# Attention: four of ten chunks of probabilities turned in 32x32 squares by VectorE and put in place by transfers on chip

## The chip, the cores and the metric

The kernel runs on one core of a Trainium2 chip, in fp32 throughout. The metric is the device time of one execution in microseconds (us). The time before is 2645.14 us, the median of three runs (2643.16 to 2648.54). Five engines work side by side, each with a queue of its own: TensorE (PE, with its weight loads as PEld), VectorE (DVE), ScalarE (ACT), GpSimd (POOL) and SyncE (SP), which here only issues transfers (DMAs). They meet in semaphores.

## The reference

A layer norm, then attention and a feed-forward layer with low-rank additions, summed onto the input:

```python
B, S, H = 4, 512, 1024;  NH, NKV, D = 32, 8, 128;  G = NH // NKV        # G = 4
xn = layernorm(x)
q, k, v = split(xn @ w_qkv)                    # 32 query heads, 8 key/value heads
scores = einsum('bqhgd,bkhd->bhgqk', q, k) * D ** -0.5
bias = where(rel >= 0, -slopes * sqrt(rel), -inf)     # causal, by the root of the distance
attn = softmax(scores + bias)
out = einsum('bhgqk,bkhd->bqhgd', attn, v)
x = x + out @ w_o + (xn @ W.T + b + routed_low_rank(xn))
```

What matters here is that `attn` is computed with the queries on the partitions (the softmax sums over keys, along the free dimension), while the product with `v` sums over keys and so wants the keys on the partitions. The probabilities have to be turned.

## The kernel before

There are three stages. `project` makes q, k and v (its two outer levels of products use fewer multiplications by sums of blocks) and leaves them in HBM. `attend` does the attention. `finish` multiplies by `w_o` and `W`, takes the low-rank part and the input in, and writes out. This change is in `attend`, which runs from about 1115 to 1842 us of the profiled span.

**Units.** `attend` goes through 32 units `u = (p, h, bi)`: a pair of batch entries, a key/value head, one of the two entries. In a unit four query heads (`G`) are handled together. The 512 queries are four tiles of 128 (`i` = 0 to 3), and because of the causal mask tile `i` needs only the keys of tiles `j` = 0 to `i`. So there are 4 + 3 + 2 + 1 = 10 chunks `(i, j)` in a unit; each is 128 queries by 128 keys for four heads, 128 x 512 numbers.

**Steps.** `scores(u, i)` multiplies q and k on TensorE into a bank of PSUM (L1014). VectorE adds the bias and finds the extreme (L1019), ScalarE takes the exponential with its sum (L1023), VectorE inverts the sum (L1026) and GpSimd scales the probabilities in place (L1028). They lie in `p0` to `p3`, two buffers each. `transpose_probs(u, i)` turns every chunk of tile i: four turns on TensorE (L1039), 128 x 128 each, into one PSUM bank, and one copy to a `pt` buffer, by VectorE for even j (L1042) and by ScalarE for odd j (L1044). `weigh(u, i)` multiplies the turned chunks with v (L1052), and ScalarE copies the result to `o` (L1053).

**Order.** The loop over units runs one unit ahead with the scores. In the loop of unit u, TensorE does, for i = 3, 2, 1, 0, the scores of tile i of the *next* unit, then (for i = 1 and 0) the weighing of tile i + 2 of u, then the turns of tile i of u. At i = 2 it also turns the next unit's v (`values`, L1003). At the end come the weighings of tiles 1 and 0. TensorE's order is the order of the program (`manual_schedule(engines={PE})`). On the other engines, SP's queue included, a scheduler orders the instructions by its own estimate of when each can run; only instructions in `pin` keep their order among themselves.

**Transfers.** SP's queue issues for each unit the loads of k, q and v two units ahead (L973 to L975) and, spread over two units, the stores of `o`, of sums of `o` and of `ot` for the last stage (`middle_sums`, L1105 to L1119). The sums `os` and `ot` are made by VectorE and GpSimd (L130, L133).

**Buffers.** SBUF is laid out by hand: `counts` and `sizes` name how many buffers of which size a tag has, one if nothing is said. `homes[0]` is the first home of the next stage's operands; it is open already while the attention runs, and its tile `s1` (5 x 256 numbers on each partition) is not in use by then.

Of the kernel before, what the change touches and what calls it, by code (L numbers as in the profile page):

```python
# [12 lines left out]
F32 = mybir.dt.float32  # L13
# [8 lines left out]
P = 128  # L22
NH, NKV, D = 32, 8, 128
G = NH // NKV
# [41 lines left out]
def kernel(  # L66
# [13 lines left out]
    nc = tc.nc  # L80
    B, S, H = x.shape
# [5 lines left out]
    HS = S // 2  # L87
    SCALE = D ** -0.5
    KB = 5
# [850 lines left out]
            assert not (soon or later or weights or quiet or any(apart))  # L940


    def attend(front, begin):


        early = pool("bq", side="right")
        with ExitStack() as stack:
            sb, sq = None, early.__enter__()
            units = [(p, h, bi) for p in range(NP) for h in range(NKV) for bi in range(2)]
            sizes = {"dist": (S,), "q": (G, S), "k": (S,), "vT": (S,), "bias": (G, S)}  # L950
            counts = {"q": 2, "k": 2, "vT": 2, "v": 2, "pt": 10, "o": 4, "ot": 2}
            for i in (3, 2, 1, 0):
                sizes[f"p{i}"] = (G, (i + 1) * P)
                counts[f"p{i}"] = 2
            sizes.update(v=(NT, D), pt=(S,), os=(3, 2, S), o=(G, S), ot=(9, HS))
            queries = ("dist", "q", "k", "vT", "bias")

            def buf(tag, name):
                where = sq if tag in queries else sb
                return where.tile([P, *sizes[tag]], F32, tag=tag, name=name, bufs=counts.get(tag, 1))  # L960

            Q, K, VT, V, PR, O, bias = {}, {}, {}, {}, {}, {}, {}

            def label(u):
                return "_".join(str(k) for k in u)

            def load(u, queue=nc.sync):
                p, h, bi = u
                n = label(u)
                K[u] = buf("k", f"k_{n}")  # L970
                Q[u] = buf("q", f"q_{n}")
                VT[u] = buf("vT", f"vT_{n}")
                queue.dma_start(out=K[u], in_=k_d[2 * p + bi, h - h % 2][:, h % 2])  # L973
                queue.dma_start(out=Q[u], in_=q_d[2 * p + bi, h])
                queue.dma_start(out=VT[u], in_=v_d[2 * p + bi, h - h % 2][:, h % 2])  # L975
# [11 lines left out]
                out=dist, in_=dist, compare_op=ALU.is_ge, fill=FAR,  # L987
# [10 lines left out]
            def values(u):  # L998
                n = label(u)
                V[u] = buf("v", f"v_{n}")  # L1000
                tr = bank("tr", f"v_{n}")
                for t in range(NT):
                    nc.tensor.transpose(tr[:, ts(t, P)], VT[u][:, ts(t, P)], ident)  # L1003
                nc.scalar.copy(V[u], tr.rearrange("p (t d) -> p t d", d=D))

            def scores(u, i):
                p, h, bi = u
                n = (i + 1) * P
                m = f"{label(u)}_{i}"
                tot = sb.tile([P, G], F32, tag=f"tot{i}", name=f"tot_{m}", bufs=2)  # L1010
                pr = PR[u, i] = buf(f"p{i}", f"p_{m}")
                for g in range(G):
                    sc = bank("sc", f"{m}_{g}")
                    nc.tensor.matmul(  # L1014
                        sc[:, :n], Q[u][:, g, ts(i, P)], K[u][:, :n], start=True, stop=True
                    )

                    low = sb.tile([P, 1], F32, tag=f"low{g}", name=f"low_{m}_{g}", bufs=2)
                    nc.vector.tensor_tensor_reduce(  # L1019
                        pr[:, g], sc[:, :n], bias[p, h][:, g, S - n :], -SCALE, BIG,  # L1020
                        ALU.add, ALU.min, low,
                    )
                    nc.scalar.activation(  # L1023
                        pr[:, g], pr[:, g], AF.Exp, bias=low, scale=-1.0, accum_out=tot[:, g : g + 1]
                    )
                nc.vector.reciprocal(tot, tot)  # L1026
                for g in range(G):
                    nc.gpsimd.tensor_scalar(  # L1028
                        pr[:, g], pr[:, g], tot[:, g : g + 1], 1.0, ALU.mult, ALU.mult
                    )  # L1030

            PT, OS = {}, {}

            def transpose_probs(u, i):
                for j in range(i + 1):
                    m = f"{label(u)}_{i}_{j}"
                    tr = bank("tr", m)
                    for g in range(G):
                        nc.tensor.transpose(tr[:, ts(g, P)], PR[u, i][:, g, ts(j, P)], ident)  # L1039
                    pt = buf("pt", f"pt_{m}")  # L1040
                    if j % 2 == 0:
                        nc.vector.tensor_copy(pt, tr)  # L1042
                    else:
                        nc.scalar.copy(pt, tr)  # L1044
                    PT[i, j] = pt
# [95 lines left out]

            for tag in "ot os o p3 p2 p1 p0 v pt".split():
                buf(tag, f"lay_{tag}")
            for i in (3, 2, 1, 0):
                scores(units[0], i)
                if i == 3:
                    values(units[0])
            for n, u in enumerate(units):
                p, h, bi = u
                nxt = units[n + 1] if n + 1 < len(units) else None  # L1150
                after = units[n + 2] if n + 2 < len(units) else None
                if after:
                    load(after)
                if n == len(units) - 6:
                    front[0]()
                if not nxt:
                    early.__exit__(None, None, None)
                    front[1](O[p, h, 0])
                    fill = begin()
                if bi == 1:  # L1160
                    beside.append(middle_sums(p, h, (1, 2), "o", O[p, h, 0], True))
                for i in (3, 2, 1, 0):
                    if nxt:
                        scores(nxt, i)
                    if i > 1:
                        aside(outer, 1)
                    aside(below, 2)
                    if i < 2 or not nxt and i < 3 or n == close - 2 and i == 2:
                        aside(beside, 2)
                    if i < 2:  # L1170
                        weigh(u, i + 2)
                        if i == 0 and not nxt:
                            outer_sums(p, h, slice(HS, S))
                        next(fill, None)
                    transpose_probs(u, i)
                    next(fill, None)
                    if i == 2 and nxt:
                        values(nxt)
                    if i == 3:
                        aside(outer, 1)  # L1180
                    if not nxt:
                        if i == 3:
                            aside(beside, 2)
                        if i == 2:
                            while beside:
                                aside(beside, 1)
                        if i < 2:
                            front[3 - i]()
                if after and after[2] == 0:
                    distances(after)  # L1190
                aside(beside, 2)
                weigh(u, 1)
                next(fill, None)
                weigh(u, 0)
                if n == close:

                    while beside:
                        aside(beside, 1)
                for _ in fill:
                    pass  # L1200
                if bi == 1:
                    if n + 1 == close:
                        o = O[p, h, 1]
                        outer.append(outer_steps(p, h))
                        aside(outer, 1)
                        t = OS[p, h]
                    else:
                        o, t = outer_sums(p, h, slice(0, HS if (p, h) == last else S))
                        beside.append(pause(3))
                        for k in range(2):  # L1210
                            O.pop((p, h, k))
                        OS.pop((p, h))
                    below.append(middle_sums(p, h, (7, 4), "o", o, False))
                    beside.append(middle_sums(p, h, (5, 6, 3), "os", t, False))
# [427 lines left out]
    homes, begun = [], {}  # L1642
# [36 lines left out]
    with tc.manual_schedule(engines={PE, SP}):  # L1679
        attention = attend(  # L1680
            (
                lambda: bring(0, "w", *QUARTERS[:3]), second_home,
                lambda: (ops[1].weights(1), ops[1].weights(2)), lambda: ops[1].tokens(1),
            ),
            begin,
        )
        project(lambda: next(attention))
    with tc.manual_schedule(engines={PE}):
# [42 lines left out]
```

## Time and profile before

| what | value |
| --- | --- |
| median of three runs | 2645.14 us (2643.16 to 2648.54) |
| profiled execution, its own device time | 2642.97 us |
| its span, from the first to the last instruction | 2641.2 us |
| granted TensorE clock, mean | 0.999 |
| TensorE turns of probabilities (L1039) | 1280, 167.6 us busy |
| VectorE copies of turned chunks (L1042) | 192, 683 ns each |
| data moved by transfers | 656.19 MB, 248 GB/s over the span |

How to read such lines: in the list of busy time each engine has its busy microseconds, its share of the span and its number of instructions. In the table of stretches come the stretch, its length, the busy time and instructions (x) of PE, PEld, DVE, ACT and POOL, the granted clock, the share of the transfer engines in use and GB/s. A line of groups is: source line, engine, operation, what is written <- what is read, shape, count, then busy us and mean ns of one, then the idle time of the engine just before them and who ended it. A line of waits reads "who waited <- for whom: us in total, times, longest". A line of a timeline is: start, length, engine, source line, operation; "SPq" is SP's queue, and its length is the time that the issue held SP, not the time of the transfer. A matmul in fp32 shows as two instructions, a turn as one. The busy time of TensorE's groups is modelled at the ends, so neighbouring groups overlap by some tenths of a microsecond.

### The profile page before, as it was taken

To read this page: it belongs to the slowest core of one execution; us is meant where nothing else is said; L and a number is where in the kernel's file an instruction comes from. 1 tells how busy PE (TensorE), PEld (TensorE's weight loads), DVE (VectorE), ACT (ScalarE), POOL (GpSimd) and SP (SyncE) were. 2 spreads that over 40 slices of the span, in tenths; PEclk is the share of its full clock that TensorE was granted. 3 is DMA by queue.
4 is the path that set the end of the run, shared out by engine and by line. 5 is a ranking of instruction groups with operands and counts; after the bars stand their busy time and mean duration, and the time that the engine had idled before them with its cause. 6 is when DMAs were issued, how large, how long until landed. Compare 5 with 4: busy or idle time off the path is not lost.

```text
span 2641.2 us, 35979 instructions
## 1 busy us (share of the span) xinstructions
PE 2592.3 (98%) x11872; PEld 2069.8 (78%) x11872; DVE 1799.8 (68%) x3654; ACT 651.7 (25%) x1730; POOL 1924.0 (73%) x1976
## 2 busy tenths in 40 slices
PE   7999999999999999999999999999999999999999
PEld 6888888888888888856666665656788888888887
DVE  7776867867676677656666666676766666656574
ACT  3111111100000000366766766665000000000000
POOL 3687888877898988666877777684765566755593
PEclk9999999999999999999999999999999999999999
DMA  4479897869876776436566666757987878878884
GB/s 148 135 268 309 305 316 258 275 200 330 275 261 216 240 255 207 144 105 223 189 222 215 209 223 195 233 208 240 369 276 285 310 294 318 296 275 310 308 329 164
DMA packets 386570, 656.19 MB, mean 248 GB/s; under 512 B 22441, under 2 KB 291113, under 8 KB 376274
## 3 DMA queue, kind: packets, MB, share of 16 engines
q1 hardware_dynamic: 314322, 566.47, 61.8%
q10 hardware_dynamic: 70752, 82.85, 9.7%
q0 software_dynamic: 1312, 4.59, 0.5%
q8 instruction: 95, 1.56, 0.2%
q14 instruction: 89, 0.73, 0.1%
HBM read 392.72 MB, written 261.10 MB: 248 GB/s over the span
## 4 chain that ended last, share of the span: by engine, by line
PE 67%; POOL 3%; DVE 3%; DMA 2%; issue 1%; SPq 0%; ACT 0%; POOLq 0%; DVEq 0%; ACTq 0%
PE pc L1310 16%; PE psc L1014 9%; PE po L1052 9%; PE pd L1310 8%; PE pc_q L553 6%; PE pa L1310 4%; PE pc_kv L553 3%; PE ptr L1039 3%; PE pd_q L553 3%; PE pd_kv L553 2%; PE pa_q L553 1%; DVE p L1019 1%; DVE pt L1042 1%; PE pa_kv L553 1%; DMA s<-os 1%
## 5 line engine op out<-in xcount | busy, mean ns | idle before, releaser
L1028 POOL TENSOR_SCALAR p<-p,tot 128x256 f32<-128x256 f32 (+3 forms) x512 | 320.5, 648 | 136.8 <-DVE tot L1026 87.3
L1014 PE MATMUL psc<-k,q 128*128 128x512 f32 (+3 forms) x1024 | 306.2, 437 | 3.4 <-DVE low L1019 2.1
L1019 DVE CUSTOM_DVE_ANT_0 p<-psc,bias 128x256 f32<-128x256 f32 (+3 forms) x512 | 244.6, 490 | 93.6 <-PE psc L1014 71.2
L1023 ACT ACTIVATE p<-p,low 128x256 f32<-128x256 f32 (+3 forms) x512 | 283.8, 555 | 74.6 <-DVE low L1019 61.3
L1052 PE MATMUL po<-pt,v 128*128 128x512 f32 x640 | 290.9, 593 | 0.5 <-DVE pt L1042 0.5
L133 POOL TENSOR_TENSOR t<-w 128x640 f32<-128x640 f32 x95 | 186.3, 1961 | 135.6 <-DMA w<-m 58.9
L1014 PEld LDWEIGHTS psc<-k,q 128*128 128x128 f32 x1024 | 172.6, 190 | 102.7 <-issue 54.3
L133 POOL TENSOR_TENSOR t<-w,t 128x640 f32<-128x640 f32 x95 | 197.3, 2077 | 34.2 <-PE pc L1310 30.5
L1039 PEld LDWEIGHTS ptr<-ident,p 128*128 128x128 f32 x1280 | 147.3, 141 | 71.4 <-issue 40.1
L1052 PEld LDWEIGHTS po<-pt,v 128*128 128x128 f32 x640 | 116.6, 190 | 109.6 <-issue 99.6
L133 POOL TENSOR_TENSOR wr<-wr 128x256 f32<-128x256 f32 x220 | 173.1, 789 | 33.2 <-DMA wr<-in_w_o_dram 10.3
L1042 DVE COPY pt<-ptr 128x512 f32<-128x512 f32 x192 | 130.0, 683 | 75.8 <-PE ptr L1039 73.8
L1039 PE MATMUL ptr<-ident,p 128*128 128x128 f32 x1280 | 167.6, 274 | 4.3 <-DVE pt L1042 2.9
L553 PE MATMUL pc_q<-xi,ti_q 128*128 128x256 f32 x640 | 165.7, 381 | 2.9 <-DVE q L130 1.8
L168 ACT COPY m<-pc 128x256 f32<-128x256 f32 x30 | 11.2, 373 | 562.7 <-PE pc L1310 488.7
L133 DVE TENSOR_TENSOR wr<-wr 128x256 f32<-128x256 f32 x220 | 141.8, 645 | 7.6 <-DMA wr<-in_w_o_dram 4.0
L133 POOL TENSOR_TENSOR ti_q<-w_q 128x256 f32<-128x256 f32 x128 | 106.1, 829 | 56.0 <-PE pc_kv L553 32.9
L553 PEld LDWEIGHTS pc_q<-xi,ti_q 128*128 128x128 f32 x640 | 119.6, 190 | 24.5 <-issue 7.8
L553 PE MATMUL pd_q<-xi,ti_q 128*128 128x256 f32 x448 | 116.0, 381 | 5.6 <-POOL ti_q L133 5.6
L1310 PE MATMUL pc<-sa,w 128*128 128x256 f32 x480 | 113.8, 385 | 4.5 <-DMA sa<-s 4.5
L168 ACT COPY q<-pc_q 128x256 f32<-128x256 f32 x64 | 23.8, 372 | 357.1 <-PE pc_q L553 309.1
L1310 PE MATMUL pd<-s,w 128*128 128x256 f32 x480 | 111.5, 379 | 0.4 <-DVE s L133 0.4
(343 smaller groups left out, 6003.5 us busy)
## 6 DMA issues: line engine op xcount, KB each, us to landing
sa<-s SPq DMA_DIRECT2D x98, 640.0 KB, 8.1
s<-ot SPq DMA_DIRECT2D x107, 384.0 KB, 4.8
m<-wr SPq DMA_DIRECT2D x70, 512.0 KB, 4.7
w<-m SPq DMA_DIRECT2D x28, 1280.0 KB, 7.2
w_q<-in_w_qkv_dram SPq DMA_DIRECT2D x16, 2048.0 KB, 12.2
q<-q SPq DMA_DIRECT2D x32, 1024.0 KB, 7.2
s<-os SPq DMA_DIRECT2D x45, 512.0 KB, 4.8
t<-wr SPq DMA_DIRECT2D x40, 512.0 KB, 4.2
```

The lines of the kernel that those rows point to most:

```text
L133: return eng.tensor_tensor(dst, u, v, ALU.subtract)
L168: nc.scalar.copy(dst, src)
L553: nc.tensor.matmul(dst, ops_w[m][:, c, :], XI[i][m][:, c, :], start=start and c == 0, stop=c == 1, skip_group_check=True,)
L1014: nc.tensor.matmul(sc[:, :n], Q[u][:, g, ts(i, P)], K[u][:, :n], start=True, stop=True)
L1019: nc.vector.tensor_tensor_reduce(pr[:, g], sc[:, :n], bias[p, h][:, g, S - n :], -SCALE, BIG, ALU.add, ALU.min, low,)
L1023: nc.scalar.activation(pr[:, g], pr[:, g], AF.Exp, bias=low, scale=-1.0, accum_out=tot[:, g : g + 1])
L1028: nc.gpsimd.tensor_scalar(pr[:, g], pr[:, g], tot[:, g : g + 1], 1.0, ALU.mult, ALU.mult)
L1039: nc.tensor.transpose(tr[:, ts(g, P)], PR[u, i][:, g, ts(j, P)], ident)
L1042: nc.vector.tensor_copy(pt, tr)
L1052: nc.tensor.matmul(po, V[u][:, j, :], PT[i, j], start=(j == 0), stop=(j == i))
L1310: nc.tensor.matmul(bk, w[:, k], x[:, k], start=start and k == 0, stop=stop and k == KB - 1, skip_group_check=True,)
```

## The change

Four of the ten chunks of a unit no longer go through TensorE: `(3, 0)`, `(3, 2)`, `(2, 0)` and `(2, 2)`. All four were copied out of PSUM by VectorE. Instead `turn_apart` has VectorE turn each 32 x 32 square of the chunk where it stands, from `p` into a tile `px` (borrowed from `s1` in `homes[0]`; one buffer, shared by tiles 3 and 2). That leaves every square turned inside, but the squares of a 128 x 128 block still stand in the old places. `place_apart` moves the squares: for each pair (a, b) of four groups of 32 partitions, one transfer on SP's queue, from the partitions of a in `px` to those of b in `pd3` or `pd2`: 16 transfers of 32 partitions x 1 KB, each with both chunks and all heads. `weigh` then reads the chunk in `pd` in runs of 32 numbers; v and the sums are as before. The buffers `pt` fall from ten to six, and `pd3` and `pd2` (4 KB a partition each, one buffer each) take their room.

For tile 2 of unit u, both steps come after TensorE's turns at i = 3 of the same loop; it is weighed at i = 0. For tile 3 of the next unit, the turn comes at i = 1 and the placing at i = 0 of the loop before; it is weighed at i = 1 of its own loop. The first unit's tile 3 is done ahead of the loop.

```diff
-    def attend(front, begin):
+    def attend(front, begin, homes):
...
-            counts = {"q": 2, "k": 2, "vT": 2, "v": 2, "pt": 10, "o": 4, "ot": 2}
+            counts = {"q": 2, "k": 2, "vT": 2, "v": 2, "pt": 6, "o": 4, "ot": 2}
...
+            apart = {3: (0, 2), 2: (0, 2)}
+            SQ = 32
+            for i, js in apart.items():
+                sizes[f"pd{i}"] = (P // SQ, len(js), G, SQ)
...
-            PT, OS = {}, {}
+            PT, OS, ahead = {}, {}, {}
+
+            def turn_apart(u, i):
+
+                js = apart[i]
+                px = homes[0].tile([P, KB, HS], F32, tag="s1", name=f"px_{label(u)}_{i}")
+                px = px.rearrange("p k c -> p (k c)")[:, : len(js) * S].rearrange(
+                    "p (b n g i) -> p b n g i", n=len(js), g=G, i=SQ
+                )
+                for n, j in enumerate(js):
+                    nc.vector.transpose(
+                        out=px[:, :, n],
+                        in_=PR[u, i][:, :, ts(j, P)].rearrange("p g (b c) -> p b g c", c=SQ),
+                    )
+                ahead[u, i] = px
+
+            def place_apart(u, i):
+                px = ahead.pop((u, i))
+                pd = buf(f"pd{i}", f"pd{i}_{label(u)}")
+                for a in range(P // SQ):
+                    for b in range(P // SQ):
+                        nc.sync.dma_start(
+                            out=pd[ds(b * SQ, SQ), a], in_=px[ds(a * SQ, SQ), b]
+                        )
+                for n, j in enumerate(apart[i]):
+                    ahead[u, i, j] = pd[:, :, n].rearrange("p a g i -> p g a i")
 
             def transpose_probs(u, i):
                 for j in range(i + 1):
+                    if (u, i, j) in ahead:
+                        PT[i, j] = ahead.pop((u, i, j))
+                        continue
...
                 scores(units[0], i)
                 if i == 3:
                     values(units[0])
+                if i == 2:
+                    turn_apart(units[0], 3)
+                    place_apart(units[0], 3)
...
                     transpose_probs(u, i)
+                    if i == 3:
+                        turn_apart(u, 2)
+                        place_apart(u, 2)
+                    if nxt and i == 1:
+                        turn_apart(nxt, 3)
+                    if nxt and i == 0:
+                        place_apart(nxt, 3)
```

More of the change, by code (lines that the diff above doesn't have):

```diff
@@ L1143, in attend @@
                 buf(tag, f"lay_{tag}")
+            for i in apart:
+                buf(f"pd{i}", f"lay_pd{i}")
             for i in (3, 2, 1, 0):
@@ L1684 @@
             ),
-            begin,
+            begin, homes,
         )
```

## The prediction

> **What bounds the kernel now.** I read the page's busy shares first, then busy time by stretch for the attention stage (1120 to 1840 us) and two of its loops, then who waited for whom on TensorE there, then the groups of the turned lines, then the timelines of TensorE and of SP's queue.
>
> ```profile
> PE 2592.3 (98%) x11872; PEld 2069.8 (78%) x11872; DVE 1799.8 (68%) x3654; ACT 651.7 (25%) x1730; POOL 1924.0 (73%) x1976
> ...
> 1120.00:1840.00 720.00, 712.81 (x3029) 436.35 (x3028) 485.99 (x1431) 483.43 (x1337) 521.35 (x616) 1.00 0.63 205
> 1413.63:1436.46 22.83, 22.64 (x98) 13.90 (x97) 17.11 (x49) 14.59 (x41) 13.86 (x21) 1.00 0.84 265
> 1436.46:1459.31 22.85, 22.71 (x97) 13.84 (x96) 13.84 (x44) 16.60 (x45) 21.11 (x19) 1.00 0.46 151
> ...
> PE ptr L1039 <- DVE pt L1042: 2.9, 15, 0.2
> PE psc L1014 <- DVE low L1019: 2.1, 4, 0.9
> ```
>
> TensorE is busy 99% of the attention stage and waits 5.0 us in 720. A loop over one unit takes 22.84 us and is TensorE's own work end to end; there are 32. So time taken off TensorE is gained, as long as nothing else needs more than the shortened loop.
>
> ```profile
> L1039 PE MATMUL ptr<-ident,p 128*128 128x128 f32 x1280 | 167.6, 274 | 4.3 <-DVE pt L1042 2.9
> L1042 DVE COPY pt<-ptr 128x512 f32<-128x512 f32 x192 | 130.0, 683 | 75.8 <-PE ptr L1039 73.8
> ...
> 1439.89 2.22 PE L1039 MATMUL ptr<-ident,p 128*128 128x128 f32 x16
> 1441.94 2.75 PE L1014 MATMUL psc<-k,q 128*128 128x384 f32 x8
> 1444.53 1.47 PE L1039 MATMUL ptr<-ident,p 128*128 128x128 f32 x12
> 1445.95 0.66 PE L1003 MATMUL ptr_v<-ident,vT 128*128 128x128 f32 x4
> ```
>
> Sixteen turns (i = 3) take 1439.89 to 1441.94, 2.05 us; twelve (i = 2) take 1.42 us. SP's queue in a loop of the same kind:
>
> ```profile
> 1428.91 0.36 SPq L1118 DMA_DIRECT2D s<-os  x1
> 1429.32 0.51 SPq L1119 DMA_DIRECT2D s<-ot  x1
> 1429.87 1.03 SPq L1118 DMA_DIRECT2D s<-os  x1
> 1431.23 0.84 SPq L1119 DMA_DIRECT2D s<-ot  x1
> 1432.12 1.30 SPq L1118 DMA_DIRECT2D s<-os  x1
> 1433.47 1.25 SPq L1119 DMA_DIRECT2D s<-ot  x1
> ...
> L975 SPq DMA_DIRECT2D vT<-v x29: 319/332/935, 1126.9 to 1767.0; - x29
> DMA to landing us min/median/max: 2.5/3.1/6.6
> ...
> SPq L1118 <- POOL o L133: 172.5, 15, 19.5
> SPq L1116 <- DMA w<-in_w_o_dram: 3.4, 1, 3.4
> ```
>
> An issue takes SP 0.32 us[...], over 1 us behind others, and about 0.05 us lies between two. The last line is a store that waits for a load it shares no data with: counted in the trace, the hardware-queue issues signal on eight semaphores in turn, some 158 each, and each waits for the semaphore it will use. A ninth transfer cannot start before the first has landed.
>
> **TensorE, removed.** Half of the turns of i = 3 (1.03 us) and two thirds of i = 2 (0.95) go: 1.98 us a unit, 63 us over 32 units (by the group's mean, 512 x 167.6/1280 = 67). The loop would be 20.86 us. What TensorE adds: the weighing reads those four chunks in runs of 32 elements. Nothing in the trace has such a moving operand; the ends are nothing and, at half rate, 4 x 0.91 us (290.9/320) a unit. I take nothing, the L1052 row itself: same type, same count. A chunk also now comes from 16 transfers on eight semaphores; TensorE's semaphore instructions take 51 ns each in this trace, so up to 8 x 51 ns twice a unit, 0.8 us, 26 us over the stage. Waiting instructions can pass while the previous matmul (0.45 us) runs: I take 0, and keep 26 us for the range.
>
> **VectorE.** Four evictions of 0.683 us go, four square turns 128x512 come. The trace has no such turn. Nearest rows: the L1042 copy, 0.683, and a 128x512 tensor_tensor between buffers, 0.67 to 0.74. The Trainium skill (VectorE: DVE Perf Modes, "The three transpose paths") gives 311 ns for 128 columns of a 2-byte type; four of those are 1.24 us. By the rows VectorE changes by nothing; by the page it gains 2.2 us of work a unit, 19.3 of 20.9 us in its busier loop (17.1 now). I take 0.69 and keep the other end.
>
> **SP, added: 32 issues a unit**, two placings of 16 transfers, 32 KB each, 32 rows of 1 KB. Issue price: a one-row transfer took 0.285 us (L1400), 128 rows 0.32; I take 0.32 + 0.05. That is 5.9 us a placing, 11.8 us a unit. SP spent 8.4 and 9.8 us issuing between the vT loads at 1400.96, 1423.92 and 1446.64, so SP goes from 9.1 to 20.9 us a unit, where TensorE wants 20.86. [...]the old issues could shrink toward 11 x 0.37 = 4.1 us, so 16 to 21. SP's order is the scheduler's: it serves one queue, and behind a waiting placing stand the loads and stores of k, q, vT, o, os, ot; behind a store that waits for POOL (up to 19.5 us above) stand the placings.
>
> **Landing.** No transfer on chip is in the trace. The quickest near row is vT, 2.5 us from issue, median 3.1; stores land after 4.8 (s<-ot). I take 2.5 to 3.1 for the last of a placing. With eight in flight, 0.37 us apart, the ninth is due 2.96 us after the first: just free at 2.5, not at 4.8, where a transfer would need 0.6 us. The Trainium skill speaks against the change here (DMA: Bandwidth & Descriptors, "Rules for kernel authors": coalesce, transfers under 64 KB pay mostly overhead) with a fixed 2 us a transfer ("Anatomy of one DMA", for the gpsimd path). Were they paid one by one, 32 x 2 = 64 us a unit, impossible to hide; the trace's issues 0.4 us apart show that they overlap, so my sum uses issue time and one landing. The data is small: 1024 packets of 1 KB a unit at 46 ns (median in the trace) over 16 engines is 2.9 us; the share 0.63 to 0.65 now (14.8 us a loop) makes that 17.7 of 20.9.
>
> **The new ring of waits.** One source tile px serves both placings, so per unit: turn 3 (two turns, 1.4 us), place 3, turn 2, place 2, turn 3 of the next. Each half is 1.4 + 5.9 + 2.5 = 9.8 us, the ring 19.6 (20.8 at 3.1 us), with no other SP work in its way. Walking it beside TensorE's shortened loop: turn 3 needs POOL's p of 512 columns, which ends 8.6 to 13.3 us into a loop (1422.2 and 1404.1, loops from 1413.63 and 1390.8); place 3 then runs to about 20 us and lands near 23, 2 us into the next loop; turn 2 and place 2 land at 12; weighing i = 2 wants it at 15. Slack 3 us. Into that fall, every second loop, six stores of 1428.91 to 1434.72 (5.8 us) on top of place 3, four more (2.8) and k, q (1.4 to 2.6) on top of what follows. Two units are 39.2 us of ring plus 8 to 11 us of such issues that cannot move aside: 47 to 50, 23.6 to 25.1 a unit. I take 24.2: 1.35 us over today's 22.84, times 31 loops, +42 us. VectorE waits for px in its own order: behind a waiting turn stand the reductions of the next scores, and TensorE stops when its three score banks are full. That is what is late next: TensorE at L1052 for pd, or at L1014 for VectorE.
>
> The ends: the first unit's place 3 has eight us of cover before its weighing; the last unit's place 2 falls beside the big loads of the next stage (0 to 10 us). I take 0.
>
> **The sum.** Own time of the profiled execution 2643.0 (span 2641.2), 2.2 below the median 2645.1. On the median: 2645 + 42 = 2687.
>
> **The rivals.** (a) *Hidden: the transfers stay in the slack.* For it: SP idles 59% now, and loads and stores have room of a loop or more; the ring alone is 19.6. Then the loop is 20.9 to 21.6: gain 1.3 to 2.0 us x 32, 40 to 63 us, 2582 to 2605. Against: SP would have to run 97% full in order. (b) *Even*: the ring closes at 22.7 to 22.95, within 5 us of 2645. (c) *VectorE blocked and landings late*: landings at 4.8 us make 0.6 us a transfer, half a ring 1.4 + 9.6 + 4.8 = 15.8, ring 31.6 alone; with half the placings so, 26 to 28 a unit: +100 to +160, 2745 to 2805. The point between gain and loss is a ring of 22.84 us: 3.2 us of foreign issues or late landing per unit beyond the bare 19.6.
>
> **How the numbers follow.** Likeliest, the ring with stores in its way: 0.50, 2655 to 2740, at 2687. (c) 0.15. (a) 0.28. (b) 0.07. A measurement of this kernel tells about 0.2%, 5 us. Faster 0.28, same 0.07, slower 0.65. The range reaches down into (a) and up into (c): 2592 to 2780.
>
> **What would show it.** Right: L1039 falls to 768, L1042 to 64; a loop longer than 22.84 us; TensorE's waits for pd (L1052) or for VectorE's low (L1014) grow from 5 us to 100 and more in the stage; SP issuing about 20 us a loop; placings landing 2.5 to 5 us after their last issue. Wrong: a loop near 20.9 us with TensorE still at 99% (a), which the slack in SP's order would explain; or turns near 1.2 us, with VectorE the full engine; or L1052's pace above 0.455 us an instruction, the runs of 32.

## The result and the profile after

The changed kernel takes 2979.13 us (2977.8 to 2980.85, four runs) beside 2645.04 us of the kernel before: ratio 1.1262, 95% interval 1.1242 to 1.1281. It is 334 us slower; 2687 was forecast, with 2780 as the upper end. The direction was right. The size was not, and neither was what the sum was built on: a ring of waits through `px`, where in the runs SP's queue is full.

Lines of the page after (busy time and the groups of the new lines), then the attention stage as a stretch (in the columns of the table before), and last the weighing in the kernel before. The weighing is now L1085 (L1052 before), the square turns L1047, the placing L1058.

```profile
PE 2620.0 (88%) x11360; PEld 2043.9 (69%) x11360; DVE 1778.0 (60%) x3654; ACT 636.7 (21%) x1730; POOL 1892.9 (64%) x1976
...
L1085 PE MATMUL po<-pd,v 128*128 128x512 f32 x256 | 185.4, 816 | 281.1 <-DMA pd<-px 281.1
L1085 PE MATMUL po<-pt,v 128*128 128x512 f32 x384 | 217.7, 680 | 0.0
L1047 DVE STREAM_TRANSPOSE px<-p 128x512 f32<-128x512 f32 x128 | 83.6, 691 | 213.8 <-DMA pd<-px 171.4
...
1120.00:2170.00 1050.00, 742.11 (x2523) 412.64 (x2522) 472.43 (x1445) 472.22 (x1352) 502.44 (x624) 0.86 0.56 176
...
L1052 PE MATMUL po<-pt,v 128*128 128x512 f32 x640 | 290.9, 593 | 0.5 <-DVE pt L1042 0.5
```

The stage is 1050 us in place of 720. TensorE's work fell by 512 turns (63 us by the prediction's count), yet it is *busy* for longer, 742.1 us for 712.8, and idle for 308 us where it had been idle for 7. So 301 us of waiting and 92 us of slower running stand against 63 us saved: 330 of the 334 us. The slower running shows in the granted clock, 0.86 in the stage, and in the weighing's instructions, 816 and 680 ns on average for 593 before.

The chain of what released what, in two loops of the stage (start, length, what):

```profile
by line: SPq L1058 31.3%; PE po L1085 20.9%; DMA vT<-v 19.7%; PE psc L1019 11.1%; DMA pd<-px 5.2%; issue 3.7%; PE ptr L1072 2.5%; SPq L979 1.7%; SPq L1149 1.5%; SPq L1152 1.4%; SPq L978 1.1%
...
1525.88 0.59 SPq L1058
1526.51 1.83 DMA pd<-px
1528.43 5.05 PE po L1085 x6
```

One issue after another holds SP for 0.59 us, the next begins 0.04 to 0.05 later; the last one lands in 1.83 us; then TensorE may weigh. SP's and TensorE's timelines over the same loop, and the line of the placing:

```profile
1515.30 11.80 SPq L1058 DMA_DIRECT2D pd<-px  x16
1527.21 0.52 SPq L1151 DMA_DIRECT2D s<-o  x1
1527.77 0.51 SPq L1152 DMA_DIRECT2D s<-ot  x1
1528.32 1.03 SPq L1151 DMA_DIRECT2D s<-o  x1
1529.39 1.13 SPq L1152 DMA_DIRECT2D s<-ot  x1
1530.63 11.31 SPq L1058 DMA_DIRECT2D pd<-px  x16
...
1518.49 1.27 PE L1019 MATMUL psc<-k,q 128*128 128x128 f32 x8
1528.43 2.05 PE L1085 MATMUL po<-pd,v 128*128 128x512 f32 x2 [8.67 <-DMA pd<-px]
...
L1058 SPq DMA_DIRECT2D pd<-px x1024: 507/589/2322, 1119.2 to 2172.1; - x171
DMA to landing us min/median/max: 1.7/1.8/12.9
...
SPq L1058 <- DMA q<-q: 17.2, 14, 2.1
```

SP has hardly a gap: placing, stores, placing. A placing takes 10.0 to 11.8 us of its time, two of them and the other issues (about 9 us a loop, as before) make some 30 us. The two loops here are 37.9 and 27.9 us long, 32.8 on average over the stage. All of SP's waits come to 63 us in the 700 from 1300 to 2000, and the last line is the longest of them. The placing's wait for a load of q, with which it shares no data, fits the eight semaphores of which the prediction speaks; with other such loads it comes to 28.5 us, 4% of the time.

### The profile page after: what moved, and what is told of

Same layout as the page of the kernel before. It is cut to its first block, busy times and chain, and to the rows that moved or that the text cites. A ratio compares the mean times of both kernels' runs of the same rounds, so it can differ in the third digit from the quotient of the medians.

```text
span 2976.0 us, 36294 instructions
## 1 busy us (share of the span) xinstructions
PE 2620.0 (88%) x11360; PEld 2043.9 (69%) x11360; DVE 1778.0 (60%) x3654; ACT 636.7 (21%) x1730; POOL 1892.9 (64%) x1976
## 4 chain that ended last, share of the span: by engine, by line
PE 50%; SPq 17%; DMA 7%; POOL 2%; issue 2%; DVE 1%; ACT 0%; DVEq 0%; POOLq 0%
PE pc L1355 14%; SPq L1058 13%; PE pd L1355 7%; PE po L1085 6%; PE pc_q L553 6%; DMA vT<-v 4%; PE pa L1355 4%; PE pc_kv L553 3%; PE pd_q L553 3%; PE psc L1019 2%; DMA pd<-px 2%; PE pd_kv L553 1%; PE pa_q L553 1%; SPq L1152 1%; PE pa_kv L553 1%
## 5 line engine op out<-in xcount | busy, mean ns | idle before, releaser
L1033 POOL TENSOR_SCALAR p<-p,tot 128x256 f32<-128x256 f32 (+3 forms) x512 | 295.7, 596 | 402.1 <-DVE tot L1031 402.1
L1085 PE MATMUL po<-pd,v 128*128 128x512 f32 x256 | 185.4, 816 | 281.1 <-DMA pd<-px 281.1
L1085 PEld LDWEIGHTS po<-pd,v 128*128 128x128 f32 x256 | 60.1, 255 | 343.6 <-issue 203.9
L1085 PE MATMUL po<-pt,v 128*128 128x512 f32 x384 | 217.7, 680 | 0.0
L1047 DVE STREAM_TRANSPOSE px<-p 128x512 f32<-128x512 f32 x128 | 83.6, 691 | 213.8 <-DMA pd<-px 171.4
L133 POOL TENSOR_TENSOR wr<-wr 128x256 f32<-128x256 f32 x220 | 172.7, 787 | 33.4 <-DMA wr<-in_w_o_dram 10.1
L1086 ACT COPY o<-po 128x512 f32<-128x512 f32 x128 | 74.9, 585 | 489.8 <-PE po L1085 489.8
L1075 DVE COPY pt<-ptr 128x512 f32<-128x512 f32 x64 | 44.1, 690 | 175.6 <-PE ptr L1072 175.4
L1085 PEld LDWEIGHTS po<-pt,v 128*128 128x128 f32 x384 | 82.0, 220 | 96.9 <-issue 87.0
L1072 PEld LDWEIGHTS ptr<-ident,p 128*128 128x128 f32 x768 | 96.1, 146 | 70.2 <-issue 51.7
```

What stands on the lines that cost most here:

```text
L133: return eng.tensor_tensor(dst, u, v, ALU.subtract)
L1033: nc.gpsimd.tensor_scalar(pr[:, g], pr[:, g], tot[:, g : g + 1], 1.0, ALU.mult, ALU.mult)
L1047: nc.vector.transpose(out=px[:, :, n], in_=PR[u, i][:, :, ts(j, P)].rearrange("p g (b c) -> p b g c", c=SQ),)
L1085: nc.tensor.matmul(po, V[u][:, j, :], PT[i, j], start=(j == 0), stop=(j == i))
L1086: nc.scalar.copy(O[u][:, :, ts(i, P)], po.rearrange("p (g k) -> p g k", k=P))
```

## The experiments

Line numbers differ by a few between kernels. All edits are to the changed kernel, except for the last control.

### Is it the issue, the bytes, or the ring through px?

A source tile of its own for tile 3:

```diff
+            sizes["px"] = (4, HS)
...
-                px = homes[0].tile([P, KB, HS], F32, tag="s1", name=f"px_{label(u)}_{i}")
+                if i == 3:
+                    px = buf("px", f"px_{label(u)}_{i}")
+                else:
+                    px = homes[0].tile([P, KB, HS], F32, tag="s1", name=f"px_{label(u)}_{i}")
```

> Tile 3 gets a source tile of its own (4 KB on each partition, in the room of the queries); tile 2 keeps the borrowed one. Same 32 transfers a unit. Theory A (SP's queue is full: an issue from SBUF to SBUF holds SP for 0.59 us and the next starts 0.05 later, 32 x 0.634 = 20.3 us a unit beside 9.4 us of other issues, so the loop is about 30 to 33 us): nothing to gain, 2920 to 2985 us. Theory R (the ring of waits through the single px, as in the prediction): the ring is cut, the loop falls toward TensorE's 20.9 to 23 us, 2590 to 2700 us.

Measured: 2967.86 us (one run). Cutting the ring gives 11 us of 334. The ring through px, around which the prediction had built its sum, is not what holds the loop while SP is full.

Half of the bytes by the same number of transfers:

```diff
-            apart = {3: (0, 2), 2: (0, 2)}
+            apart = {3: (0,), 2: (0,)}          # pt: 8 buffers
```

> One chunk per tile ((3,0) and (2,0)) instead of two: the same 32 transfers a unit with the same waits, each 32 rows of 512 B instead of 1 KB; 8 of the 16 turns go back to TensorE and two copies to VectorE. Theory A: SP's time is by the issue, so the loop stays at 30 to 33 us: 2900 to 2985 us. Theory B: half of the bytes, half of the loss, 2780 to 2850 us.

Measured: 2962.57 us (one run). With half of the bytes, and 8 of the 16 turns back on TensorE, the time is the same within 17 us; an issue still takes 589 ns in the median:

```profile
L1058 SPq DMA_DIRECT2D pd<-px x1024: 507/589/2077, 1115.7 to 2156.2; - x171
```

SP's time is by the issue, not by the byte.

The same bytes by a quarter of the transfers. This leaves out the placing itself: the squares stay on their partitions.

```diff
-                for a in range(P // SQ):
-                    for b in range(P // SQ):
-                        nc.sync.dma_start(
-                            out=pd[ds(b * SQ, SQ), a], in_=px[ds(a * SQ, SQ), b]
-                        )
+                for a in range(P // SQ):
+                    nc.sync.dma_start(out=pd[:, a], in_=px[:, a])
```

> The same bytes from px to pd, but in four transfers of 128 partitions x 1 KB instead of sixteen of 32 partitions; the squares stay on their partitions, so the placing itself is left out. 8 issues a unit. Theory A: SP 8 x about 0.5 + 9.4 = 13.4 us a unit, SP free again, TensorE the bound at 20.9 to 21.5: 2583 to 2605 us. Theory B: the same bytes, so about 2950 to 2985 us. Theory R: the ring becomes 2 x (1.4 + 2 + 2) = 10.8 us, also 2583 to 2605.

Measured: 2780.33 us, ratio 1.0519 (1.0501 to 1.0536). 199 of the 334 us go with 24 of 32 issues: theory B falls, theory A is right in kind. But 2583 to 2605 had been expected. Something else holds another 175 us or more.

Tile 3 alone:

```diff
-            apart = {3: (0, 2), 2: (0, 2)}
+            apart = {3: (0, 2)}                 # pt: 8 buffers; no placing of tile 2
```

> Only chunks (3,0) and (3,2) are turned by VectorE and placed; tile 2 goes through TensorE as before. 16 transfers a unit. Theory A: SP 10.1 + 9.4 = 19.5 us a unit, below TensorE's 21.8; TensorE saves 1.03 us a unit, so 2612 to 2650 us, depending on what SP's order delays. Theory B (what costs is the bytes on the way and their landing, not the issues): half of the loss is left, about 2790 to 2830 us.

Measured: 2726.57 us, ratio 1.032 (1.0304 to 1.0335). Half of the issues remove three quarters of the loss, so it isn't proportional to issues (theory B's half is refuted too), and yet 2612 to 2650 had been expected. SP, at 19.5 us a unit by the sum, is not free enough. Its own waits, and TensorE's for `pd`, between 1200 and 1800 us:

```profile
SPq L1151 <- POOL o L133: 56.7, 11, 8.6
SPq L1151 <- DVE os L133: 35.0, 11, 4.0
...
PE po L1085 <- DMA pd<-px: 44.9, 18, 4.4
```

For 92 us in 600 SP stands at stores whose sums are not ready, and what comes behind them stands too.

### What holds the wide version?

In the wide run TensorE no longer waits for `pd`, but for VectorE. Who waited for whom between 1200 and 1800 us, and on SP's queue:

```profile
PE psc L1019 <- DVE low L1024: 108.8, 36, 7.6
DVE px L1047 <- DMA pd<-px: 82.4, 17, 7.2
DVE px L1047 <- POOL p L1033: 32.9, 21, 3.1
...
SPq L1148 <- POOL o L133: 132.6, 11, 12.9
```

Read upward: SP's queue stands at a store of `o` until GpSimd has summed it; behind it stands a placing; VectorE's next turn waits for that placing to release px; behind the turn stand the reductions of the scores; and TensorE waits for those. Two edits to the wide version, one for each link: a px of its own for tile 3, by the same lines as above, and GpSimd's stores on GpSimd's queue:

```diff
-                queue = nc.gpsimd if (p, h) == last and not kept else nc.sync
+                queue = nc.gpsimd if not kept and ((p, h) == last or of == "o") else nc.sync
```

> The four wide transfers of the run before (the placing itself left out: squares stay on their partitions) and a px of its own for tile 3. Theory V (with SP free, what is left of the loss is the shared px: a placing of tile 3 stands in SP's order behind stores of o that wait for GpSimd, the turn of tile 2 waits for px in VectorE's order, and TensorE waits for VectorE's low): the wait falls away, TensorE saves 1.98 us a unit, 2583 to 2630 us. Theory W (VectorE's or ScalarE's work or the loads are late for another reason): it stays near 2780.

> The four wide transfers (placing itself left out), one px, but the stores of o and ot that GpSimd's sums feed are issued by GpSimd's own queue, so that no transfer on SP stands behind them. GpSimd pays 4 issues of 0.75 to 0.83 us in two units. Theory V: SP's waits for GpSimd (132.6 us in 600) go, VectorE's waits for px shrink, 2583 to 2650 us. Theory W: near 2780 us, or more by GpSimd's issues (up to 50 us).

Measured: px of its own 2758.41 us, ratio 1.0431 (1.0415 to 1.0446); the stores on GpSimd's queue 2673.24 us, ratio 1.0108 (1.0093 to 1.0123). Both lie above the range of theory V. Taking the stores off SP removes 107 us of what was left, px by itself 22. With px of its own, VectorE's wait changed its name rather than its length:

```profile
DVE px L1051 <- POOL p L1034: 109.5, 46, 7.5
```

Both at once:

> Two placings of four wide transfers (the placing itself left out), two px tiles, GpSimd's stores on its queue: all three suspects removed at once. Theory V (VectorE's wait for px is what was left at 2673 us): 2585 to 2640 us. If VectorE's turn of tile 3 waits for GpSimd's p instead (the turn is asked for in the same loop in which p is scaled), it stays at 2660 to 2690.

Measured: 2756.54 us, ratio 1.0427 (1.0412 to 1.0443), no better than px alone and 83 us worse than the queue alone. The edits don't add: with two px tiles the scheduler puts the turn of tile 3 earlier into VectorE's order, and there it waits 110.7 us in 600 for GpSimd's p. In the loop below it stands before the last reductions of 256 columns; with the queue alone it stood behind them.

```profile
1439.72 1.30 DVE L1051 STREAM_TRANSPOSE px<-p 128x512 f32<-128x512 f32 x2 [6.40 <-POOL p L1034]
1440.94 0.38 DVE L1025 CUSTOM_DVE_ANT_0 p<-psc,bias 128x256 f32<-128x256 f32 x1
```

The expectation's second half named this wait; its 2660 to 2690 us missed what the wait costs.

### Real placings with fewer issues

All chunks of tile 3 and none of tile 2, one placing a unit with rows of 2 KB:

```diff
-            apart = {3: (0, 2), 2: (0, 2)}
+            apart = {3: (0, 1, 2, 3)}           # px 8 KB in the queries' room, pt: 5 buffers
```

> All four chunks of tile 3 and none of tile 2: the same four of ten chunks, but one placing a unit of 16 transfers with rows of 2 KB, px of 8 KB of its own in the queries' room, five pt buffers. SP 16 x 0.634 + 9.4 = 19.5 us a unit, as with tile 3 alone; TensorE saves 2.05 us (loop 20.8), VectorE makes four turns and saves two copies (+1.4 us a unit). Theory A alone (SP's time is the limit and is now below TensorE's): 2585 to 2640. With theory V as well (a placing of 10 us stands behind stores that wait): the placing lands late for the weighing at 9.65 us of the loop, as with tile 3 alone (2727): 2680 to 2760 us.

Measured: 2727.61 us, ratio 1.0307 (1.029 to 1.0325). SP's issues alone don't set it (theory A by itself would give 2640 or less). They fill 81% of the time between 1200 and 1800 us, and SP waits for another 104 us, 75.5 of them at stores that need GpSimd's sums. The placing lands late in every second loop. TensorE's timeline shows what a late landing costs; below the gap are stretches from the first two weighings, with the granted clock in the third column from the end:

```profile
1406.29 6.71 PE L1086 MATMUL po<-pd,v 128*128 128x512 f32 x8 [4.42 <-DMA pd<-px]
1431.24 3.67 PE L1086 MATMUL po<-pd,v 128*128 128x512 f32 x8 [1.00 <-ACT p L1029]
1457.07 5.23 PE L1086 MATMUL po<-pd,v 128*128 128x512 f32 x8 [4.44 <-DMA pd<-px]
...
1406.30:1408.80 2.50, 2.50 (x3) 1.14 (x4) 2.46 (x4) 0.00 (x0) 0.47 (x2) 0.50 1.03 320
1431.20:1434.70 3.50, 3.46 (x8) 1.58 (x9) 1.33 (x3) 0.38 (x2) 3.50 (x5) 1.00 1.02 312
```

The same eight instructions take 3.67 us after a wait of 1.00 us, and 5.23 to 6.71 after one of 4.4. After the long wait the granted clock is 0.50, after the short one 1.00. The transfer engines are as full in both stretches, so it isn't their load that slows TensorE. A wait of that length is paid for about one and a half times.

Through HBM, one store and four loads in place of sixteen transfers:

```diff
+                xd = x_d[i]
+                nc.sync.dma_start(out=xd, in_=px)
+                back = xd.rearrange("(a c) b n g i -> c b a n g i", c=SQ)
+                for b in range(P // SQ):
+                    nc.sync.dma_start(out=pd[ds(b * SQ, SQ)], in_=back[:, b])
```

> The placing goes through HBM: px is stored whole by one transfer (128 rows of 4 KB) and brought back by four (32 rows of 4 x 1 KB each), 10 issues a unit in place of 32; px of its own for tile 3. SP 10 x 0.45 + 9.4 = 14 us a unit. Landing: a store 4 to 5 us, a load 3 to 4, about 9 us a placing in place of 12. The transfer engines carry 2 MB more a unit (about 5.5 us of all sixteen; 20 of 20.9 us). Theory A: SP free, 2600 to 2680 us. Theory B (bytes): twice the bytes of the changed kernel, so no better than 2950 us.

Measured: 2884.33 us, ratio 1.0907 (1.089 to 1.0923), outside both ranges. SP is light (its issues fill 47% of the stage), but a placing is now two landings in a row, 6.6 us for the store and 3.5 for a load in the median, with SP standing between them, and SP's order again holds the loads of the next unit behind waits. TensorE waits more for VectorE than for `pd` here, and VectorE for GpSimd's p, which is taken up below (1200 to 1800 us):

```profile
DVE px L1052 <- POOL p L1035: 89.2, 29, 8.2
PE psc L1021 <- DVE low L1026: 87.0, 30, 8.3
PE po L1090 <- DMA pd<-x_d: 58.6, 10, 6.4
```

How much of the loss each of them makes is not shown. The run also prices the issue: the loads here have 32 partitions, as the placing had, and read HBM. Below the gap are the wide transfers from SBUF to SBUF, with 128 partitions.

```profile
L1065 SPq DMA_DIRECT2D pd<-x_d x256: 302/431/1522, 1122.5 to 2076.7; - x128
...
L1057 SPq DMA_DIRECT2D pd<-px x256: 465/607/1559, 1119.7 to 1963.9; - x128
```

Like with like in these traces: an issue right behind another of its own line took 431 ns from HBM and 589 from SBUF to SBUF, both with 32 partitions; after a pause of over 0.5 us, 319 and 507. The wide ones took 607 in the median. So it is not the 32 partitions that make the placing's issue dear. The transfer on chip costs 0.16 to 0.19 us more in these runs, and standing one behind another 0.08 to 0.11. Why is not shown.

The single placing with GpSimd's stores on its own queue, and then with four stores on ScalarE's as well:

> One placing a unit (all four chunks of tile 3, 16 transfers with rows of 2 KB), and the stores of o and ot that GpSimd's sums feed on GpSimd's own queue. Theory O (what is left in the single placing is order: every second loop the placing stands behind a store that waits for GpSimd, lands 4.4 us late, and TensorE then runs its next eight matmuls in 5.2 to 6.7 us instead of 3.6): about 7 us in two loops go, 2727 - 16 x 7 = 2615; 2595 to 2660 us. Theory S (SP still has too much to issue in a loop, 19 of 21 us): the placing is late all the same, 2690 to 2740 us.

> As before, and the four stores of o that are kept (two units) are issued by ScalarE. SP has 4 issues fewer in two loops (about 4 us), ScalarE pays 4 x 0.4 us in two loops. Theory O: no further change, 2595 to 2660. Theory S: a further 20 to 60 us faster than the run without it.

Measured: 2774.99 us, ratio 1.0493 (1.0478 to 1.0509), and 2786.32, ratio 1.0542 (1.0526 to 1.0558). Both slower than without; both theories missed. The trace of the first shows the in-order wait elsewhere (1200 to 1800 us):

```profile
DVE ot L130 <- DMA s<-ot: 93.8, 11, 9.3
```

A store of `ot` now stands behind the placing, VectorE waits for its buffer, and the scores' reductions wait behind that. Taking a load off SP without controlling the order moved the wait to another engine.

### GpSimd's p

The single placing by wide transfers (placing left out) with GpSimd's stores on its queue:

> One placing a unit of four wide transfers of 2 KB rows (the placing itself left out), GpSimd's stores on its queue. SP 4 x 0.6 + 9.4 - 1.6 = 10 us a loop. It has all of TensorE's saving and none of the issue price: theories O and S both give 2585 to 2620 us; above 2640 something beyond SP (VectorE's four turns, GpSimd's p) still holds the loop.

Measured: 2726.33 us, ratio 1.0309 (1.0291 to 1.0326). SP's issues fill 46% of the time here, so the last clause holds: something beyond SP. The timelines of GpSimd, VectorE and TensorE in one loop, with who waited, and below the gap TensorE's and VectorE's waits between 1200 and 1800 us:

```profile
1423.97 2.37 POOL L130 TENSOR_TENSOR os<-o 128x1024 f32<-128x1024 f32 x1 [2.91 <-DMA s<-os]
1426.42 2.37 POOL L133 TENSOR_TENSOR o<-o,o 128x1024 f32<-128x1024 f32 x1
1428.75 2.37 POOL L133 TENSOR_TENSOR os<-os,o 128x1024 f32<-128x1024 f32 x1
1431.20 2.34 POOL L133 TENSOR_TENSOR os<-o,os 128x1024 f32<-128x1024 f32 x1
1433.52 2.70 POOL L1034 TENSOR_SCALAR p<-p,tot 128x512 f32<-128x512 f32 x4
...
1436.25 0.71 DVE L1048 STREAM_TRANSPOSE px<-p 128x512 f32<-128x512 f32 x1 [6.09 <-POOL p L1034]
...
1438.00 1.22 PE L1020 MATMUL psc<-k,q 128*128 128x256 f32 x2 [5.83 <-DVE low L1025]
...
PE psc L1020 <- DVE low L1025: 81.4, 20, 8.5
DVE px L1048 <- POOL p L1034: 76.9, 18, 6.8
```

In every second loop GpSimd makes four sums before it scales tile 3. Before the change nobody wanted that tile until the next loop; now VectorE turns it in the same one, and waits with everything behind it. The loops are 21.7 and about 29.5 us long in turn. To bring p forward, the sums were asked for after the next unit's scores of tile 3 (`settle` holds the old call):

```diff
                     if nxt:
                         scores(nxt, i)
+                    if i == 3 and owed:
+                        ph = owed.pop()
+                        o, t = settle(*ph)
...
+                    elif n + 2 < close:
+                        owed.append((p, h))
+                        continue
                     else:
-                        o, t = outer_sums(p, h, slice(0, HS if (p, h) == last else S))
...
+                        o, t = settle(p, h)
```

> As the single placing by four wide transfers (the placing itself left out, GpSimd's stores on its queue, 2726 us), but the four sums of o on GpSimd that follow every second unit (9.5 us) are asked for after the next unit's scores of tile 3 instead of before, so that GpSimd scales p of tile 3 first. Theory G (what is left without SP's load is VectorE's turn of tile 3 waiting for GpSimd's p, with the reductions of the scores behind it): TensorE's wait of about 6 us and its slow start in every second loop go, 2726 - 16 x 8 = 2598; 2585 to 2640 us. If not G: 2700 to 2740 us.

> As the two placings by wide transfers with GpSimd's stores on its queue (2673 us; placing left out), with the same later sums. Theory G: VectorE's wait for p (38.9 us in 600) goes, 2600 to 2650 us. If not G: 2660 to 2690 us.

> The real single placing (four chunks of tile 3, 16 transfers of 2 KB rows on SP, all stores on SP; 2728 us) with the later sums. GpSimd's sums come about 3 us later, so the stores that wait for them do as well. Theory S (the placing of 11 us and what stands around it in SP's order are the limit): 2690 to 2760 us. Theory G alone: 2600 to 2660 us.

> The kernel before with the later sums alone, as a control: TensorE is busy 99% of the stage and p of tile 3 is not wanted before the next loop, so nothing is to gain; 2640 to 2660 us under every theory.

Measured: 2749.78 us (ratio 1.0396, 1.038 to 1.0411), 2716.47 (1.0272, 1.0257 to 1.0287), 2713.75 (1.0259, 1.0241 to 1.0278) and, as the control, 2644.13 (0.9999, 0.9989 to 1.0008). The first two are misses: slower than without the edit. Their traces say that the edit didn't do what it was for. The scheduler kept the sums ahead of p and even put two sums of `ot` between, so that p came later still, and TensorE's wait grew to 7.75 us in the loop below (the first of the two runs):

```profile
1443.33 1.26 POOL L130 TENSOR_TENSOR ot<-o 128x512 f32<-128x512 f32 x1
1444.66 1.26 POOL L133 TENSOR_TENSOR ot<-ot,o 128x512 f32<-128x512 f32 x1
1445.90 4.93 POOL L1034 TENSOR_SCALAR p<-p,tot 128x512 f32<-128x512 f32 x8
...
1449.71 1.22 PE L1020 MATMUL psc<-k,q 128*128 128x256 f32 x2 [7.75 <-DVE low L1025]
```

A later p with a longer time fits theory G, but it doesn't settle it. The real placing is 14 us better with the edit, the best of the real placings, and stays within theory S's range; why it gains is not shown.

So the dependence itself was taken away, by leaving out GpSimd's scaling of tile 3:

```diff
-                for g in range(G):
+                for g in range(G if i < 3 else 0):
                     nc.gpsimd.tensor_scalar(...)
```

> As the single placing by four wide transfers with GpSimd's stores on its queue (2726 us; the placing itself left out), and GpSimd's scaling of tile 3 is left out too, so that VectorE's turn of tile 3 follows ScalarE's exponential and waits for nothing of GpSimd's. TensorE's, VectorE's and SP's work is unchanged. Theory G: TensorE's wait for VectorE of about 6 us in every second loop and the slow matmuls after it go, 2585 to 2630 us. If GpSimd's p is not the cause: 2700 to 2740 us.

> As the real single placing (16 transfers of 2 KB rows on SP, 2728 us), with GpSimd's scaling of tile 3 left out. Theory S (SP's order: the placing of 11 us lands late for the weighing): the turns come up to 2 us earlier, but the placing still stands behind the stores that wait for GpSimd; 2670 to 2725 us. If GpSimd's p alone were the cause: 2590 to 2630 us.

Measured: with wide transfers 2598.57 us, ratio 0.9836 (0.9819 to 0.9852); with the real placing 2694.59, ratio 1.0195 (1.0179 to 1.021). The first is the only kernel below the one before. A stretch of its stage, and TensorE's wait for VectorE between 1200 and 1700 us:

```profile
1400.00:1500.00 100.00, 97.51 (x385) 57.82 (x384) 77.23 (x229) 66.80 (x194) 69.04 (x84) 1.00 0.76 263
...
PE psc L1020 <- DVE low L1025: 2.1, 1, 2.1
```

TensorE is at 97.5% at full clock and the loop is 21.2 us long on average (weighings of tile 3 start at 1404.27, 1426.03 and 1447.17; no loop of 29 us is left). That is theory G shown: 128 us between 2726 and 2599 hang on GpSimd's p. The edit also takes 2.7 us of work a unit from GpSimd, so it doesn't tell whether p could be had in time with that work done. And the 96 us between 2695 and 2599 are the price of the real placing with all stores in SP's order: sixteen issues instead of four, together with the stores' queue, which differs between these two as well. No real version tried here beats the kernel before; the nearest took 2713.75 us.

## Why the prediction was wrong

- **TensorE's saving: right.** With SP, VectorE's wait and GpSimd's p out of the way the loop falls to 21.2 us, where 20.86 was the sum (20.79 for that kernel, which takes all sixteen turns of tile 3 off TensorE). The runs of 32 cost nothing: without a wait, the weighing from `pd` starts two instructions every 0.86 us, as the one from `pt` does (1547.23, 1548.09, 1548.95 in the changed kernel).
- **VectorE's turn: right.** 691 ns on average for 0.69 taken from the copy's row; the 1.24 us, an estimate scaled from the Trainium skill's figure for a 2-byte type (VectorE: DVE Perf Modes, "The three transpose paths"), would have been wrong by a factor of 1.8.
- **SP's issue price: the term that failed.** The sum took 0.32 + 0.05 us an issue. That was the row of vT, an issue that stands alone; the placing's stand one behind another, and go from SBUF to SBUF: 0.589 + 0.045. A unit's two placings take 20.3 us, not 11.8, and SP about 30, not 20.9. The lines in the prediction held 0.51 us for a second issue in a row, and it was passed over. The ends given for this price (0.285 to 0.32) were ends of one condition, so the range had no room for it. This is the step that failed: SP was put at 20.9 us in a loop of 20.86, just full, where it needs about one and a half loops.
- **Landing: better than taken.** 1.83 us for 2.5 to 3.1. With 1.83 us, eight in flight allow an issue every 0.23 us, so the placing's own landings don't hold it back. The eight semaphores cost it 4% of the time, where it waits for slower loads. The Trainium skill's fixed 2 us a transfer, stated for the gpsimd path (DMA: Bandwidth & Descriptors, "Anatomy of one DMA"), is near the landing, and its warning about transfers under 64 KB ("Rules for kernel authors") points the right way, but the price is in the issue: half of the bytes took the same time.
- **The ring through px: a bystander at this load.** It gave the right sign (24.2 us a loop against some 33 measured), but with a px of its own for tile 3 the kernel still takes 2968 us, 0.35 us a loop less. As far as the sign came from the ring, it was luck. The two are easily taken for each other: with 0.634 us an issue and a landing of 1.83 us, the prediction's own sum for the ring would give 31 to 32 us (an estimate: two halves of 1.4 + 10.1 + 1.8, and 4 to 5.5 of other issues), and SP's issues alone give about 30. Only the run with a second px tells them apart.
- **VectorE blocked (rival c): in part right.** It was named as what stands behind a waiting turn, and that is what holds the loop once SP is free. The late landings that gave rival (c) its size, 4.8 us, did not come: the median is 1.83. That GpSimd's p is wanted in the same loop stood in the prediction as a time (8.6 to 13.3 us into a loop), but was not counted as a wait.
- **TensorE's slow start after a wait: not foreseen.** It makes 92 us of the stage.

## What to carry to other kernels

Price a transfer's issue from rows in the same condition, back to back and between the same memories, and multiply by the count before anything else: an in-order queue at 145% of the loop settles the sign by itself. When work moves to engines that run in order, look for results that are now wanted earlier than before, since the instruction that waits for them blocks all that stands behind it, as VectorE's turn did for 6.09 us above. Taking away one wait, without control over the order, mostly moved it here.

## What the runs showed of the hardware

- An issue from SBUF to SBUF with 32 partitions held SP for 0.507 us after a pause and 0.589 behind another, whether rows had 512 B, 1 KB or 2 KB; 32-partition loads from HBM in the same place took 0.319 and 0.431.
- After long waits TensorE's next matmuls ran at half their pace (two in 2.05 us, 1.02 without a wait), for about 3 to 5 us, at a granted clock of 0.50; over the stage the clock fell to 0.86. Over the weighings of all traces here, the third instruction started 0.93 to 0.96 us after the first, full pace, after each of 27 waits of 0.5 to 1.5 us, and 1.84 to 1.87 us after it, half pace, after each of 95 waits of 4.5 us or more; between 1.5 and 4.5 us both were seen.
- VectorE turned 128x512 numbers of fp32 in squares in 691 ns, the price of a copy of the same size out of PSUM (690 in the same kernel, L1075).
